# Projecting k from f16 planes with a scale summed ahead, in a graph attention kernel

## The chip, the cores and the metric

The kernel runs on one NeuronCore of a Trainium2 chip. Five engines work from their own instruction queues, each strictly in order: TensorE (PE in the profile, its weight loads PEld), VectorE (DVE), ScalarE (ACT), GpSimd (POOL) and SyncE (SP), which issues most DMA transfers. They wait for each other through semaphores. The metric is the device time of one execution in microseconds (us); the time of a kernel is the median of its runs.

## The reference, cut to what matters

One pre-norm graph attention layer over N = 384 nodes with 1024 features, 16 heads of 64. Each of q, k and v passes two linear layers in a row, all in f32:

```python
h = jnp.maximum(_layernorm(x, axis=-1), 0.0)
q = h @ wq.T + bq
k = h @ wk.T + bk
v = h @ wv.T + bv
q2 = (q @ wiq.T + biq).reshape(N, H, D).transpose(1, 0, 2)
k2 = (k @ wik.T + bik).reshape(N, H, D).transpose(1, 0, 2)
v2 = (v @ wiv.T + biv).reshape(N, H, D).transpose(1, 0, 2)
mask = _build_mask(edge_index, edge_type, edge_type_weights, x.dtype)
scores = jnp.einsum('hnd,hmd->hnm', q2, k2) * scale + mask[None]
attn = jax.nn.softmax(scores, axis=-1)
out = jnp.einsum('hnm,hmd->hnd', attn, v2).transpose(1, 0, 2).reshape(N, OUT_F)
return x + out @ wo.T + bo
```

The mask is a 384 x 384 table, filled from 6,528 edges by scattered writes (a later edge of the same pair wins), with minus infinity where there is no edge.

## The kernel before

**Slots.** The weights come in 56 chunks of 128 x 1024 (512 KB), in the order of `chunks`: eight of Wv (slots w = 0 to 7), eight of Wq (8 to 15), eight of Wiv (16 to 23), eight of Wk (24 to 31), then Wiq and Wik by turns (32 to 47), then eight of Wo. A slot is the work on one chunk.

**Planes.** To keep f32 accuracy, an operand is kept as a high plane and a low plane (what the high one leaves out), and each product is made of three matmuls: high by high, high by low, low by high (`mm3`, lines 456 to 458). There are two kinds. Unscaled planes are fp32r (4 bytes): that is how v, q and k are projected, with `hT` (the normalised, rectified x without its division by sigma, transposed, two fp32r planes) as the moving operand. Scaled planes are f16: the matrix is multiplied by a power of two chosen so that it fits, and for that its size must be known beforehand. `scan_load` brings a chunk ahead of time into a spare buffer, `scan_sum` lets ScalarE sum its absolute values into a column of `l1`, `bound_max(w)` (VectorE) takes the largest of a row of `l1`, and `bound(w)` turns that column on TensorE (a transpose into a PSUM bank of tag "g") and lets VectorE derive the scale t and its reciprocal u (`power`). `BOUNDS` says in which slot each bound is made. Wiv, Wiq and Wo have such scales; so have v and q themselves, whose absolute sums are taken when their banks are emptied (`evac_f`).

**A slot of a projection** (`proj`). First comes `slot_head(w)`: ScalarE splits off the high plane of chunk w+2 (`split_hi`, line 107 unscaled, line 101 scaled), high planes of v or q (`planes_of`), the evacuation of the previous slot's bank (`flush`), a sum (`scan_sum`); then VectorE does `bound_max`, the low plane of chunk w+2 (`split_lo`, line 126 unscaled, line 124 scaled) and the low halves collected in `post`; then SP issues the load of chunk w+5 and the scan's load. Then TensorE does the 24 matmuls of the slot into a bank of tag "g" (three of them); after the matmuls of k = 6 `bound(w)` follows, where there is one, so that TensorE waits there for `bound_max(w)` and the later matmuls of the slot stand behind it.

**k's evacuation** (`evac_row`): VectorE multiplies the bank by `rrow`, the row of 1/sigma (line 479); ScalarE adds the bias and rounds to the high plane (line 480); VectorE makes the low plane (line 481, one slot later through `post`).

**Beside it.** VectorE compares edges with each other for the mask (`mask_detect`, `mask_index`), GpSimd scatters their values (`mask_scatter`, two a slot, 51 in all), loads the three tables back (`mask_load`, in slots 29 to 31), and adds the output bias to the residual in six pieces (`residual_add`, line 599, one in each of the slots 26 to 31, behind that slot's scatters). Neither waits for TensorE. In the k stage v2 is also scaled: its maxima (`v2_max`, line 659), a bound in slot 26 (`v2_scale`), and one evacuation a slot from slot 27 on (`v2_evac`, lines 694 and 695). In the v stage GpSimd clears `kz`, the buffer for the low planes of k2.

**After the projections** `fill_qk` does slots 32 to 47 with `qk_head` at their head; the first 84 units of it (28 k steps) run before the attention loop, the rest between its steps. The results of slots 32 and 33 are copied into stacked layouts by DMA (line 752), and then the attention's first score matmul (line 901) can go.

Of the kernel before, what the change touches and what calls it, by code (L numbers as in the profile page):

```python
# [12 lines left out]
PSC = 32768.0  # L13
BF16 = mybir.dt.bfloat16
# [12 lines left out]
def gnn_kernel(ctx: ExitStack, tc: tile.TileContext, x, edges, erows, etw, wq, wk, wv, wiq, wik, wiv, wo,  # L27
# [18 lines left out]
    WARM = (24,2,0)  # L46
# [34 lines left out]
    def weight_scale(w):  # L81
        return {"iv": u_iv, "iq": u_iq, "o": u_o}.get(chunks[w][0])
# [46 lines left out]
    SCANS = [("iv", i + 3, i + 5) for i in range(8)] + [("iq", i + 13, i + 15) for i in range(8)]  # L129
    SCANS += [("o", i + 25, i + 27) for i in range(8)]  # L130

    def scan_buf(i):
        return scan[:, i % 3, :] if i < 16 else qF3[:, i % 3, :]

    def scan_load(w):
        for i, (n, at, _) in enumerate(SCANS):
            if at == w:
                nc.sync.dma_start(scan_buf(i), W[n][i % 8])

    def scan_sum(w):  # L140
        for i, (n, _, at) in enumerate(SCANS):
            if at == w:
                x = scan_buf(i)
                nc.scalar.activation(x, x, AF.Abs, accum_out=l1[:, 1 + i // 16, i % 8:i % 8 + 1])
# [7 lines left out]
    BOUNDS = {8: 0, 13: 1, 16: 2, 23: 3, 37: 4}  # L152

    def bound_of(w):
        return ((0, t_v, u_v), (1, t_iv, u_iv), (0, t_q, u_q), (1, t_iq, u_iq), (2, t_o, u_o))[BOUNDS[w]]

# [39 lines left out]
    w8, vmax = small[:, 4:16], small[:, 16:24]  # L196
    t_v, u_v, t_iv, u_iv, t_v2, u_v2, t_o, u_o, t_sum, u_sum, t_out = (small[:, c:c + 1] for c in range(24, 35))
    bias_ao, bias_q = small[:, 40:48], small[:, 48:56]
    t_q, u_q, t_iq, u_iq, u_c, neg_c = (small[:, c:c + 1] for c in (35, 36, 37, 38, 39, 56))
    l1 = const.tile([128, 3, 8], F32, name="l1")  # L200
# [276 lines left out]
    def evac_row(ps, hi, lo, bias):  # L477
        f = work.tile([128, N], F32, tag="e", name="f", bufs=EB)
        nc.vector.tensor_tensor(f, ps[:, :N], rrow, OP.mult)
        nc.scalar.activation(hi, f, AF.Identity, bias=bias)  # L480
        post.append(lambda: nc.vector.scalar_tensor_tensor(lo, f, bias, hi.bitcast(F32), op0=OP.add, op1=OP.subtract))
# [22 lines left out]
    def slot_head(w):  # L504
# [3 lines left out]
        if w > 16:  # L508
            planes_of(w - 17, qT, qF, u_q)
# [18 lines left out]
    def proj(src, dst, bidx, extra=None):  # L528
        nonlocal w
        for m in range(8):  # L530
# [22 lines left out]
            else:  # L553
                pend.append(lambda ps=ps, m=m: evac_row(ps, dst[:, 0, m, :], dst[:, 1, m, :],
# [567 lines left out]
```

## Time and profile before

| | |
|---|---|
| time, median of 3 runs | 283.77 us (283.31 to 285.13) |
| profiled execution | 284.17 us |
| its span, first to last instruction | 282.5 us |
| mean granted TensorE clock | 0.999 |
| ScalarE busy | 197.6 us (70%) |
| GpSimd busy | 145.7 us (52%) |
| bytes moved by DMA | 65.69 MB |
| absolute sums of scanned chunks on ScalarE | 16 at 1044 ns and 8 at 1051 ns |

Rows of the profile have this form: line of the kernel, engine, operation, the tile written <- the tiles read, shape, count; then busy time, the mean of one in ns, and the idle time of that engine just before with what ended it. In a timeline the first column is the start and the second the duration, in us. Busy time of TensorE overstates it, since matmuls are pipelined: the distance from one start to the next is what a matmul costs in a stream.

### The profile page before, as it was taken

The numbers are of one execution on the slowest core, as the hardware profiler recorded it, in microseconds if no ns is written. First come the engines' busy times: TensorE is split into PE (matmuls) and PEld (weight loads), VectorE is DVE, ScalarE is ACT, GpSimd is POOL, SyncE is SP. The second block draws the span as 40 slices with busy tenths as digits, with TensorE's granted clock in tenths as the row PEclk, the third lists the DMA queues.
The fourth block names the chain that finished last, engine by engine and source line by source line (L and its number), as shares of the span: only waits on it lengthen the run. The fifth ranks groups of instructions, "written<-read, shape, count | busy, mean of one in ns | idle before, by whom it ended". The sixth has DMA issues, their size and how long they took to land. (4 is left out here: it accounts for less than half of the span.)

```text
span 282.5 us, 5050 instructions
## 1 busy us (share of the span) xinstructions
PE 275.7 (98%) x1630; PEld 218.0 (77%) x1630; DVE 222.4 (79%) x515; ACT 197.6 (70%) x393; POOL 145.7 (52%) x170
## 2 busy tenths in 40 slices
PE   7999999999999999999999999999999999999994
PEld 6899999999954447999977887878778695655443
DVE  3948965885869754999989987898988889999423
ACT  3786887795989644243986878687888897777510
POOL 3857565458778676899003435447373732332210
PEclk9999999999999999999999999999999999999999
DMA  7799999999668841477993689999988989522105
GB/s 265 235 319 404 372 387 404 342 363 338 243 216 303 319 134 62 149 277 224 363 353 76 212 261 225 231 223 194 213 203 190 227 227 255 113 69 48 35 19 206
DMA packets 45562, 65.69 MB, mean 233 GB/s; under 512 B 26592, under 2 KB 32224, under 8 KB 45536
## 3 DMA queue, kind: packets, MB, share of 16 engines
q1 hardware_dynamic: 43152, 63.18, 72.9%
q0 software_dynamic: 2064, 1.80, 2.3%
q10 hardware_dynamic: 320, 0.39, 0.5%
q8 instruction: 13, 0.21, 0.3%
q14 instruction: 13, 0.11, 0.1%
HBM read 50.36 MB, written 3.39 MB: 190 GB/s over the span
## 5 line engine op out<-in xcount | busy, mean ns | idle before, releaser
L456 PE MATMUL g<-g,whl 128*128 128x384 f32 (+1 forms) x312 | 105.4, 338 | 0.0
L458 PE MATMUL g<-g,whl 128*128 128x384 f32 (+1 forms) x312 | 104.0, 333 | 0.2 <-DVE whl L126 0.2
L457 PE MATMUL g<-g,whl 128*128 128x384 f32 (+1 forms) x312 | 103.8, 333 | 0.0
L313 POOL DMA_INDIRECT tab<-edge x51 | 59.5, 1167 | 31.8 <-DMA tab<-edge 14.4
L458 PEld LDWEIGHTS g<-g,whl 128*128 128x128 f32 x248 | 46.5, 188 | 0.5 <-DVE whl L126 0.5
L456 PEld LDWEIGHTS g<-g,whl 128*128 128x128 f32 x248 | 46.6, 188 | 0.4
L457 PEld LDWEIGHTS g<-g,whl 128*128 128x128 f32 x248 | 46.6, 188 | 0.0
L126 DVE TENSOR_TENSOR whl<-raw,whl 128x1024 fp32r<-128x1024 f32 x23 | 33.6, 1459 | 7.5 <-ACT whl L107 7.2
L107 ACT ACTIVATE whl<-raw 128x1024 fp32r<-128x1024 f32 (+1 forms) x38 | 33.6, 890 | 4.7 <-DMA raw<-in_wv_dram 2.2
L910 DVE CUSTOM_DVE_ANT_0 e<-s,ma,small 128x384 f32<-128x384 f32 x48 | 29.0, 606 | 1.6 <-PE s L902 1.2
L915 ACT ACTIVATE e<-e,s 128x384 f32<-128x384 f32 x48 | 29.1, 607 | 0.5 <-DVE s L910 0.4
L101 ACT ACTIVATE whl<-raw,small 128x1024 f16<-128x1024 f32 (+1 forms) x28 | 25.7, 925 | 4.1 <-PE g L458 4.0
L950 ACT ACTIVATE pt<-e,s 128x384 f16<-128x384 f32 x21 | 12.9, 612 | 17.4 <-POOL s L938 17.4
L942 POOL TENSOR_TENSOR e<-e,s 128x384 f32<-128x384 f32 x21 | 17.3, 825 | 11.9 <-DVE s L935 10.3
L124 DVE SCALAR_TENSOR_TENSOR whl<-raw,small,whl 128x1024 f16<-128x1024 f32 x16 | 21.0, 1312 | 3.0 <-ACT whl L101 2.6
L112 POOL TENSOR_TENSOR whl<-raw,whl 128x256 fp32r<-128x256 f32 x20 | 18.1, 912 | 8.7 <-ACT whl L107 8.7
L901 PE MATMUL s<-ks,qs 128*128 128x384 f32 x48 | 20.8, 433 | 0.4 <-DVE s L910 0.3
L991 POOL TENSOR_TENSOR g<-aof,g 128x384 f16<-128x384 f32 x8 | 7.4, 924 | 23.8 <-ACT g L990 23.8
L126 POOL TENSOR_TENSOR whl<-raw,whl 128x1024 fp32r<-128x1024 f32 x3 | 7.8, 2612 | 22.7 <-ACT whl L107 22.7
L456 PEld LDWEIGHTS <-g 128*128 128x128 f16 x100 | 9.8, 98 | 11.7 <-issue 3.1
L954 DVE SCALAR_TENSOR_TENSOR pt<-e,s,pt 128x384 f16<-128x384 f32 x21 | 15.7, 749 | 3.3 <-ACT pt L950 3.3
L458 PEld LDWEIGHTS <-g 128*128 128x128 f16 x100 | 9.8, 98 | 10.9
(184 smaller groups left out, 555.7 us busy)
## 6 DMA issues: line engine op xcount, KB each, us to landing
raw<-in_wv_dram SPq DMA_DIRECT2D x8, 512.0 KB
raw<-in_wq_dram SPq DMA_DIRECT2D x8, 512.0 KB
scan<-in_wiv_dram SPq DMA_DIRECT2D x8, 512.0 KB
raw<-in_wiv_dram SPq DMA_DIRECT2D x8, 512.0 KB
scan<-in_wiq_dram SPq DMA_DIRECT2D x8, 512.0 KB
raw<-in_wk_dram SPq DMA_DIRECT2D x8, 512.0 KB
raw<-in_wiq_dram SPq DMA_DIRECT2D x8, 512.0 KB
raw<-in_wik_dram SPq DMA_DIRECT2D x8, 512.0 KB
```

The source lines that it names most:

```text
L101: soon(j if parts > 1 else -1, lambda c=c: nc.scalar.activation(hi[:, c], raw[w][:, c], AF.Copy, scale=sc))
L107: soon(j if parts > 1 else -1, lambda c=c: nc.scalar.activation(hi[:, c], raw[w][:, c], AF.Copy))
L112: nc.gpsimd.tensor_tensor(lo, raw[w][:, c:c + D // 4], hi.bitcast(F32), OP.subtract)
L124: nc.vector.scalar_tensor_tensor(lo, raw[w], sc, hi, op0=OP.mult, op1=OP.subtract)
L126: (eng or nc.vector).tensor_tensor(lo, raw[w], hi.bitcast(F32), OP.subtract)
L313: nc.gpsimd.indirect_dma_start(out=tabs[c // RNG], out_offset=bass.IndirectOffsetOnAxis(ap=idx[:, c:c + 1], axis=0), in_=val[:, c:c + 1], ...
L456: nc.tensor.matmul(ps, lhi, rhi, start=first, stop=False)
L457: nc.tensor.matmul(ps, lhi, rlo, start=False, stop=False)
L458: nc.tensor.matmul(ps, llo, rhi, start=False, stop=last)
L901: nc.tensor.matmul(ps[:, :N], qs[:, o, c], ks[:, o, :], start=True, stop=False)
L910: nc.vector.tensor_tensor_reduce(e, st_ps.pop(i)[:, :N], ma[:, t, :], neg_c, 3.0e38, OP.add, OP.min, s[:, t:t + 1])
L915: nc.scalar.activation(es[i], es[i], AF.Exp, bias=s[:, t:t + 1], scale=-1.0, accum_out=s[:, 3 + t:4 + t])
```

## The change

Wk joins the matrices with a scale: its eight chunks are scanned in slots 11 to 18 and summed in slots 13 to 20, its bound is made in slot 21, and its chunks are then split into f16 planes. The scans of Wiq move from slots 13 to 20 to slots 18 to 25, its bound from slot 23 to slot 29; the bound of q moves from slot 16 to 17, the planes of q from slots 17 to 24 to slots 18 to 25, and the scan buffers are dealt out accordingly. Wo's scan keeps its slots, but its eighth load, in slot 32, is now issued too (`scan_load` in `qk_head`); before only seven were.

The moving operand becomes eight pairs of f16 planes, `hk`, of h with its division by sigma, times 1024. They are made by VectorE in slots 4 to 20 (`h_planes`): add the two planes of `hT`, multiply by 1024 and `rrow`, copy to f16, subtract for the low plane. So the bank needs no row of 1/sigma: `evac_k` reads it with ScalarE (scale and bias), copies to the high plane with ScalarE, and leaves VectorE the low plane. `hk` lies in the buffers of `nat` and `kz`; `kz` is cleared after the k projection, and the early copy of v2 goes to the tag "qs".

```diff
+HSC = 1024.0
...
-    WARM = (24,2,0)
+    WARM, H0 = (24, 2, 0), 4
...
     def weight_scale(w):
-        return {"iv": u_iv, "iq": u_iq, "o": u_o}.get(chunks[w][0])
+        return {"iv": u_iv, "iq": u_iq, "o": u_o, "k": u_k}.get(chunks[w][0])
...
-    SCANS = [("iv", i + 3, i + 5) for i in range(8)] + [("iq", i + 13, i + 15) for i in range(8)]
-    SCANS += [("o", i + 25, i + 27) for i in range(8)]
+    SCANS = sorted([(n, i + c, i + c + g, i) for n, c, g in (("iv", 3, 2), ("k", 11, 2), ("iq", 18, 2), ("o", 25, 2)) for i in range(8)], key=lambda c: c[1])
+    SROW = {"iv": 1, "k": 2, "iq": 1, "o": 2}
...
-    BOUNDS = {8: 0, 13: 1, 16: 2, 23: 3, 37: 4}
+    BOUNDS = {8: 0, 13: 1, 17: 2, 21: 5, 29: 3, 37: 4}
...
     def colmm(ps, w, src, k):
         hi, lo = whl[w]
-        mm3(ps[:, :N], hi[:, k * 128:(k + 1) * 128], lo[:, k * 128:(k + 1) * 128],
-            src[:, 0, k, :], src[:, 1, k, :], k == 0, k == KT - 1)
+        a, b = src[k] if isinstance(src, list) else (src[:, 0, k, :], src[:, 1, k, :])
+        mm3(ps[:, :N], hi[:, k * 128:(k + 1) * 128], lo[:, k * 128:(k + 1) * 128], a, b, k == 0, k == KT - 1)
...
-    def evac_row(ps, hi, lo, bias):
+    def evac_k(ps, hi, lo, bias):
         f = work.tile([128, N], F32, tag="e", name="f", bufs=EB)
-        nc.vector.tensor_tensor(f, ps[:, :N], rrow, OP.mult)
-        nc.scalar.activation(hi, f, AF.Identity, bias=bias)
-        post.append(lambda: nc.vector.scalar_tensor_tensor(lo, f, bias, hi.bitcast(F32), op0=OP.add, op1=OP.subtract))
+        nc.scalar.activation(f, ps[:, :N], AF.Identity, bias=bias, scale=s_k)
+        nc.scalar.activation(hi, f, AF.Copy)
+        post.append(lambda: nc.vector.tensor_tensor(lo, f, hi.bitcast(F32), OP.subtract))
...
         planes_of(w - 9, vT, vF, u_v)
-        if w > 16:
-            planes_of(w - 17, qT, qF, u_q)
+        if w > 17:
+            planes_of(w - 18, qT, qF, u_q)
...
         while post:
             post.pop(0)()
+        h_planes(w)
         load(w + 5)
         scan_load(w)
...
-        if w == 23:
+        if w == 21:
+            nc.vector.tensor_scalar(s_k, t_k, 1.0 / HSC, None, op0=OP.mult)
+        if w == 29:
             nc.vector.tensor_tensor(u_c, u_q, u_iq, OP.mult)
...
+    def h_planes(w):
+        k, s = divmod(w - H0, 2)
+        if s == 0 and 0 <= k < KT:
+            hs[k] = work.tile([128, N], F32, tag="e", name="hs", bufs=EB)
+            nc.vector.tensor_tensor(hs[k], hT[:, 0, k, :].bitcast(F32), hT[:, 1, k, :].bitcast(F32), OP.add)
+        if s == 1 and 0 <= k < KT:
+            nc.vector.scalar_tensor_tensor(hs[k], hs[k], HSC, rrow, op0=OP.mult, op1=OP.mult)
+        if s == 0 and 0 <= k - 1 < KT:
+            f = hs.pop(k - 1)
+            nc.vector.tensor_copy(hk[k - 1][:, 0, :], f)
+            nc.vector.tensor_tensor(hk[k - 1][:, 1, :], f, hk[k - 1][:, 0, :], OP.subtract)
...
     def extra_v(m):
-        if m in (3, 4):
-            nc.gpsimd.memset(kz.bitcast(F32)[64 * (m - 3):64 * (m - 3) + 64, :, 4 - m, :], 0.0)
         detect(m)
...
-        if m == 1:
+        if m == 2:
             vhl = big.tile([128, NT, 2 * NP, 2, 64], F16, tag="g4", name="vhl")
...
-    proj(hT, kT, 1, extra_k)
+    proj([(t[:, 0, :], t[:, 1, :]) for t in hk], kT, 1, extra_k)
     flush(True)
+    kz = work.tile([128, 2, 2, N], F32R, tag="kz", name="kz", bufs=1)
+    for j in range(2):
+        nc.gpsimd.memset(kz.bitcast(F32)[64 * j:64 * j + 64, :, 1 - j, :], 0.0)
...
         load(w + 5)
+        scan_load(w)
         scan_sum(w)
```

More of the change, by code (lines that the diff above doesn't have):

```diff
@@ L199, in gnn_kernel @@
     t_q, u_q, t_iq, u_iq, u_c, neg_c = (small[:, c:c + 1] for c in (35, 36, 37, 38, 39, 56))
+    t_k, u_k, s_k = (small[:, c:c + 1] for c in (13, 14, 15))
     l1 = const.tile([128, 3, 8], F32, name="l1")
@@ L558, in proj @@
             w += 1
[L560 removed]
+    hk = []
+    for j in range(2):
+        t = work.tile([128, 2, N], F32R, tag="nat", name="hk", bufs=2).bitcast(F16)
+        hk += [t.rearrange("p a n -> p (a n)").rearrange("p (k a n) -> p k a n", k=2, a=2)[:, k, :, :] for k in range(2)]
+    t = work.tile([128, 2, 2, N], F32R, tag="kz", name="hkz", bufs=1).bitcast(F16)
+    hk += [t.rearrange("p a b n -> p (a b n)").rearrange("p (k a n) -> p k a n", k=4, a=2)[:, k, :, :] for k in range(4)]
+    hs = {}
+    def h_planes(w):
[9 more added lines that the diff above has]
+            nc.vector.tensor_tensor(hk[k - 1][:, 1, :], f, hk[k - 1][:, 0, :], OP.subtract)
     def extra_v(m):
[L563 to L564 removed]
         detect(m)
```

23 lines of the change are left out of this document (12 added, 11 removed).

## The prediction, made before the result was known

> **What bounds the kernel now.** I read the page first, then TensorE's records in order of time, then busy time cut by slots (a slot is one weight chunk, numbered w as in the code), then the records of VectorE (DVE) and GpSimd (POOL) in the slots where TensorE stumbles, and last the chain of waits. The page and TensorE's timeline:
>
> ```profile
> span 282.5 us, 5050 instructions
> ...
> PE 275.7 (98%) x1630; PEld 218.0 (77%) x1630; DVE 222.4 (79%) x515; ACT 197.6 (70%) x393; POOL 145.7 (52%) x170
> ```
> ```profile
> 113.93 0.33 PE L456 MATMUL g<-g,whl 128*128 128x384 f32 x1
> ...
> 118.09 0.33 PE L456 MATMUL g<-g,whl 128*128 128x384 f32 x1
> ...
> 135.55 0.44 PE L458 MATMUL g<-g,whl 128*128 128x384 f32 x1 [0.17 <-DVE whl L126]
> ...
> 143.66 0.34 PE L456 MATMUL g<-g,whl 128*128 128x384 f16 x1
> ...
> 147.44 0.47 PE L456 MATMUL g<-g,whl 128*128 128x384 f32 x1
> ...
> 158.82 0.33 PE L901 MATMUL s<-ks,qs 128*128 128x384 f32 x1
> ```
>
> TensorE is never idle for long, so what counts is the step from matmul to matmul. The first two records open slots 25 and 26 of the k projection (slots 24 to 31, 24 matmuls each): 118.09 - 113.93 = 4.16 us, 173 ns a matmul in f32. The fourth and fifth open slot 32, the same 24 matmuls with f16 planes, and slot 33: 147.44 - 143.66 = 3.78 us, 158 ns. The third is a stumble in slot 30, released by VectorE's low plane of that chunk (L126). The last is the first matmul of the attention. Cut by slots 28 to 30 (columns: PE, PEld, DVE, ACT, POOL busy, clock, DMA share):
>
> ```profile
> 126.55:130.71 4.16, 4.16 (x25) 4.16 (x25) 4.16 (x3) 2.18 (x4) 4.14 (x4) 1.00 0.64 200
> 130.71:134.87 4.16, 4.16 (x25) 4.16 (x25) 4.16 (x4) 1.42 (x3) 3.65 (x4) 1.00 0.90 281
> 134.87:139.50 4.63, 4.46 (x26) 4.14 (x26) 4.63 (x8) 4.07 (x8) 0.00 (x0) 1.00 1.00 365
> ```
>
> Slot 30 takes 4.63 instead of 4.16: the stumble costs 0.5. In these slots VectorE is as full as TensorE, in the first two with three or four operations a slot. Its records say why, beside GpSimd's:
>
> ```profile
> 111.24 0.68 DVE L659 TENSOR_REDUCE small<-tv 128x1 f32<-128x512 f32 x1
> ...
> 117.68 2.94 DVE L126 TENSOR_TENSOR whl<-raw,whl 128x1024 fp32r<-128x1024 f32 x1
> 120.55 0.60 DVE L481 SCALAR_TENSOR_TENSOR g<-f,bc,g 128x384 fp32r<-128x384 f32 x1
> 121.54 1.21 DVE L126 TENSOR_TENSOR whl<-raw,whl 128x1024 fp32r<-128x1024 f32 x1
> ...
> 123.21 0.28 DVE L147 TENSOR_REDUCE small<-g 128x1 f32<-128x128 f32 x1
> ...
> 124.86 0.14 DVE L673 SCALAR_TENSOR_TENSOR small<-small 128x1 f32<-128x1 f32 x1
> ...
> 125.39 3.75 DVE L126 TENSOR_TENSOR whl<-raw,whl 128x1024 fp32r<-128x1024 f32 x1
> ...
> 135.95 0.74 DVE L695 SCALAR_TENSOR_TENSOR vhl<-s,small,vhl 128x512 f16<-128x512 f32 x1
> ...
> 140.49 1.29 DVE L124 SCALAR_TENSOR_TENSOR whl<-raw,small,whl 128x1024 f16<-128x1024 f32 x1 [0.55 <-ACT whl L101]
> ```
> ```profile
> L599 POOL TENSOR_TENSOR res<-res,bot 128x512 f32<-128x512 f32 x6 | 8.6, 1437 | 0.1
> ```
> ```profile
> 118.23 1.30 POOL L599 TENSOR_TENSOR res<-res,bot 128x512 f32<-128x512 f32 x1
> ...
> 126.07 1.30 POOL L599 TENSOR_TENSOR res<-res,bot 128x512 f32<-128x512 f32 x1
> ...
> 128.18 2.12 POOL L599 TENSOR_TENSOR res<-res,bot 128x512 f32<-128x512 f32 x1
> ...
> 133.10 1.31 POOL L599 TENSOR_TENSOR res<-res,bot 128x512 f32<-128x512 f32 x1
> ```
>
> The low plane costs 1.21 us alone, 2.94 and 3.75 when GpSimd adds the output bias to the residual meanwhile (six adds, 8.6 us, first and last at 118.23 and 133.10). VectorE loses about what the add lasts: 2.94 - 1.21 = 1.7 for 1.30; 3.75 - 1.21 = 2.5 for 1.30 and part of 2.12. Rule and row differ here. The Trainium skill (SBUF — State Buffer, "SBUF: two separate sides") says that VectorE, with two SBUF operands, and GpSimd lock one port pair, and that whoever starts first keeps it for the whole instruction. L126 started first at 117.68 and still lost, so I go by the row; the rule's own outcome is the first rival.
>
> **The change, part by part.** *Matmuls.* Eight slots from 4.16 to 3.78: 8 x 0.38 = 3.0 us, and the stumble of 0.5 goes if its cause does. That is all that TensorE can gain.
>
> *VectorE in the k projection.* The old evacuation had VectorE multiply each bank by the row of 1/sigma and make the low half; now ScalarE reads the bank and only a low half is left, about 0.60 (nearest row L481). The scaled low plane of Wk is 1.29 instead of 1.21. So VectorE gets lighter. But the bound of Wiq moves from slot 23 to slot 29, and TensorE, which works in order, does its transpose after the seventh k of slot 29. The transpose needs `bound_max(29)`, which VectorE reaches only behind everything queued ahead. From the start of slot 24 that is: six v2_max at 0.68 (4.1), low planes of chunks 26 to 30 at 1.29 (6.5), two q low planes and four low halves at 0.60 (3.6), the v2 bound and scale from 123.21 to 125.00 (1.8), two v2 low halves at 0.74 (1.5), v2_top, five small steps like those of the scale (0.7). Sum 18.2; records overlap by 0.07 (117.68 + 2.94 against 120.55), some 24 times, so 16.5. VectorE can begin when ScalarE's first copy has landed:
>
> ```profile
> 109.83 0.60 ACT L655 ACTIVATE tv<-g 128x512 f32<-128x512 f32 x1 [6.21 <-issue]
> ```
>
> 110.4 + 16.5 = 126.9, if GpSimd were silent. Adds that wait for nothing on TensorE fall where they fell: three lie wholly before 127.4 (+3.9, to 130.8), then the one of 2.12 (132.9), then the fifth (134.2), and part of the sixth. So `bound_max(29)` comes at 134.2 to 135.2. TensorE is there after five slots of 3.78, six eighths of a sixth and two transposes (0.2): slot 24 opens one f32 slot and a transpose before slot 25, at 113.93 - 4.16 - 0.1 = 109.7, and 109.7 + 18.9 + 2.8 + 0.2 = 131.6. It waits 2.6 to 3.6; I take 3.0. Behind it in TensorE's queue stand the rest of slot 29 and all that follows. In the kernel before, the same place is passed at 130.71 + 0.75 x 4.16 = 133.8; now at 134.6. The lead of 2.2 us is gone, and two slots of 3.78 instead of 4.63 and 4.16 (1.2 less) only make that good again: slot 32 opens at 134.6 + 0.9 + 7.6 + about 0.5 for a bank (next part) = 143.6, against 143.66.
>
> *ScalarE behind the moved bound.* `split_hi(32)` needs u_iq and stands in slot 30's head ahead of the evacuation of slot 29, whose bank slot 31 wants (three banks, one taken by the transpose). u_iq comes after one more low plane, two low halves and the scale: 134.7 + 1.29 + 0.60 + 0.74 + 0.9 = 138.2. From there ScalarE is full:
>
> ```profile
> 139.32 1.14 ACT L101 ACTIVATE whl<-raw,small 128x1024 f16<-128x1024 f32 x1
> ...
> 142.48 1.05 ACT L107 ACTIVATE whl<-raw 128x1024 fp32r<-128x1024 f32 x1
> ...
> 143.99 0.67 ACT L694 ACTIVATE vhl<-t,small 128x512 f16<-128x512 f32 x1
> ...
> 147.56 1.33 ACT L101 ACTIVATE whl<-raw,small 128x512 f16<-128x512 f32 x2
> ```
> ```profile
> L144 ACT ACTIVATE scan<-scan 128x1024 f32<-128x1024 f32 x16 | 16.7, 1044 | 0.0
> ...
> L466 ACT ACTIVATE nat<-g,bc 128x384 fp32r<-128x384 f32 x8 | 4.5, 564 | 1.0 <-PE g L458 1.0
> ...
> L990 ACT ACTIVATE g<-aof 128x384 f16<-128x384 f32 x8 | 4.2, 519 | 0.1
> ```
> ```profile
> 154.79 0.47 ACT nat L466
> ...
> 155.86 2.49 DMA ks<-nat
> ```
>
> Up to the split of chunk 34 (147.56 before) it has 1.14 + 1.05, three evacuations at 0.56 + 0.52 (now two passes), three v2 high halves at 0.67, two sums at 1.04 and 0.19: 9.9, less eleven overlaps of 0.09: 8.9. 138.2 + 8.9 = 147.1. The chain of waits begins there: the evacuation at 154.79 and the copy of 2.49 at 155.86 let the attention's first matmul go at 158.82, which TensorE reaches as the data land. So the entry moves by -0.5 to +0.5, and the matmuls after it are those of before.
>
> *h planes.* Eight times an add, a multiply by 1/sigma, a copy to f16 and a low plane on VectorE, in slots 4 to 20. Nearest rows: 0.60 for each two-operand step, at most 0.41 for the copy:
>
> ```profile
> L432 DVE CAST whl<-raw 128x512 fp32r<-128x512 f32 x1 | 0.4, 412 | 0.0
> ```
> ```profile
> 15.40:78.40 63.00, 63.00 (x366) 62.74 (x364) 46.18 (x147) 51.89 (x95) 37.87 (x43) 1.00 0.96 351
> 78.40:109.70 31.30, 31.30 (x149) 14.37 (x147) 20.01 (x47) 20.19 (x33) 23.06 (x23) 1.00 0.65 225
> ```
>
> 8 x 2.2 = 17.7 us, 1.0 a slot: 12.5 in the v and q stages, where VectorE has 63.0 - 46.2 = 16.8 free, 5 in the iv stage, where 11.3 are free. The low planes are queued two slots ahead, and that hides it: nothing on the path, and if the cover failed, up to the 1.0 a slot. Its side effect is that the last index of the mask comes up to 3 us later, and the scatters and adds on GpSimd with it.
>
> *Sums and loads.* Eight sums of Wk, 1.2 each, on ScalarE in slots 13 to 20 (free there: 11.1 in v and q, 11.1 in iv); those of Wiq run until slot 27. The added loads are 4 MB; five instead of three fall into the q stage, where the queues are at 0.96: 1.05 MB at 351 GB/s, 3.0 us of transfer behind loads issued three slots ahead. The eighth load of Wo is new (seven were issued), 0.5 MB in slot 32 on SP's queue ahead of the stack copies; a load takes some 1.5 us by 351 GB/s. Wk's bound at the end of slot 21 leaves two slots for two splits of 2.4. The clearing of kz goes to GpSimd after the last k matmul, ten us ahead of its use. I take nothing for any of these; uncovered, the loads would cost 1.5 to 3.
>
> **Sum.** -3.0 for the matmuls, +3.0 for the wait at the bound, -0.5 for the stumble, +0.5 for the bank: 0.0, and +-1.0 by the spread of the wait (2.6 to 3.6) and of the entry (+-0.5). The span stays at 282.5. The profiled execution took 284.17 (span and 1.7 around it), 0.4 over the median of 283.77; I state the forecast on the median: 283.8, alone 282.8 to 284.8.
>
> **Rivals.** *The gain arrives* (18%). If VectorE loses little to the adds, `bound_max(29)` is there by 131.6 and u_iq by 135. For it: 126.9 without any loss. Against it: 2.94 and 3.75. Price -3.0 and -0.5, of which the entry's chain may keep 0.2: 280.5. By the first-starter rule of the Trainium skill, cited above, the low planes would stay at 1.2 and the time would come out here; the trace does not bear it out.
>
> *The moved bound holds ScalarE* (20%), slower. Place: `split_hi(32)`. Once u_iq is later than 138.7, each us is a us at the entry, for ScalarE has no gap from there on. If each of the six adds costs 2.1 (the fourth's length) instead of 1.3, or later scatters push them behind slot 29, u_iq comes at 142: +3.4, 287.2. For it: the 3.75, and the later index. Against it: five of the six adds lasted 1.3.
>
> *The clock falls in the new wait* (8%). After the last matmuls the granted clock drops:
>
> ```profile
> 277.00:280.00 3.00, 1.61 (x15) 1.20 (x13) 0.97 (x2) 0.00 (x0) 0.00 (x0) 1.00 0.65 237
> 280.00:282.00 2.00, 0.00 (x0) 0.00 (x0) 0.00 (x0) 0.00 (x0) 0.00 (x0) 0.93 0.19 65
> ```
>
> TensorE is busy for 1.61 of the first stretch, so it ends near 278.6, and the mean over the last stretch is 0.93: at half clock that is 0.3 us, so the drop came some 3 us after the last matmul, about the length of my wait. Half speed for as long as the wait adds half of 3.0: 285.3. The Trainium skill (TensorE: Matmul & The Clock Gate, "What's actually happening") puts the idle window at about 3.4 us; by that most of my waits escape it.
>
> **Chances.** Forecast 54%, gain 18%, held ScalarE 20%, clock 8%. One per cent (2.8 us, about what a measurement of this kernel tells from no change) puts the gain into faster, forecast and clock into the same. The range 280.3 to 286.6 takes in the forecast, the clock, the gain and the start of the held case.
>
> **What would show it.** Slots 24 to 28 at 3.78. A gap of about 3 us in TensorE in slot 29, released by VectorE, with residual adds beside long low planes. ScalarE waiting in slot 30 for u_iq and full afterwards. First attention matmul at 158 to 160. Wrong: no gap in slot 29, the attention opening before 156.5, or gaps in slots 4 to 23, which would mean that the h planes have no cover.

## The result, and the profile after

The changed kernel takes 282.23 us (median of 7 runs, 281.56 to 285.85) against 283.80 (283.31 to 285.13) of the kernel before on the same chip: a ratio of 0.9932, 95% interval 0.9909 to 0.9956. In a later series on another chip it was 281.75 against 284.26, 0.9920 (0.9895 to 0.9944). So the change makes the kernel 0.7 to 0.8% faster, some 2 us, where 283.8, no change, was forecast. Medians here are over all runs; the ratios leave out runs in a slower state with a lower granted clock, such as the longest of these seven (285.85 us at 0.992). The profiled execution has a span of 280.3 us, 2.2 less than before.

From the page, the span, and among the costliest groups the scatters of GpSimd (POOL) with their idle time:

```profile
span 280.3 us, 5120 instructions
...
L316 POOL DMA_INDIRECT tab<-edge x51 | 61.7, 1210 | 40.8 <-DMA tab<-edge 27.2
```

The same group in the page of the kernel before:

```profile
L313 POOL DMA_INDIRECT tab<-edge x51 | 59.5, 1167 | 31.8 <-DMA tab<-edge 14.4
```

GpSimd now waits 27.2 us for scatters to land, before 14.4. TensorE's timeline, with the openings of slots 25, 26, 32 and 33, the transpose in slot 29 that was to wait, and the first matmul of the attention:

```profile
113.86 0.33 PE L459 MATMUL g<-hk,whl 128*128 128x384 f16 x1
...
117.76 0.33 PE L459 MATMUL g<-hk,whl 128*128 128x384 f16 x1
...
132.98 0.27 PE L167 MATMUL g<-ident,small 128*128 128x128 f32 x1
...
141.37 0.33 PE L459 MATMUL g<-g,whl 128*128 128x384 f16 x1
...
145.14 0.47 PE L459 MATMUL g<-g,whl 128*128 128x384 f32 x1
...
156.52 0.33 PE L927 MATMUL s<-ks,qs 128*128 128x384 f32 x1
```

A slot of the k projection takes 117.76 - 113.86 = 3.90 us, not 3.78. The transpose goes at once, without a wait. Slot 32 opens at 141.37 (143.66 before) and the attention at 156.52 (158.82 before): the 2.3 us won in the k stage reach the attention whole. Slots 28 to 30 by windows (columns as before):

```profile
125.67:129.56 3.89, 3.89 (x25) 2.35 (x24) 2.54 (x2) 3.86 (x8) 3.31 (x3) 1.00 0.91 331
129.56:133.57 4.01, 4.01 (x27) 2.48 (x25) 3.84 (x6) 3.88 (x8) 3.52 (x4) 1.00 0.84 297
133.57:137.47 3.90, 3.90 (x26) 2.35 (x24) 3.73 (x8) 2.36 (x4) 3.85 (x4) 1.00 0.94 315
```

No gap of TensorE in any of them; VectorE (third busy column) has 1.35 us free in slot 28. Its timeline says why, and the next two fences show GpSimd's adds and ScalarE:

```profile
127.02 2.39 DVE L125 SCALAR_TENSOR_TENSOR whl<-raw,small,whl 128x1024 f16<-128x1024 f32 x1 [2.37 <-ACT whl L102]
129.33 0.55 DVE L484 TENSOR_TENSOR g<-f,g 128x384 fp32r<-128x384 f32 x1
129.80 0.74 DVE L717 SCALAR_TENSOR_TENSOR vhl<-s,small,vhl 128x512 f16<-128x512 f32 x1
130.46 0.14 DVE L162 TENSOR_REDUCE small<-l 128x1 f32<-128x8 f32 x1
130.78 1.28 DVE L125 SCALAR_TENSOR_TENSOR whl<-raw,small,whl 128x1024 f16<-128x1024 f32 x1 [0.17 <-ACT whl L102]
131.98 1.62 DVE L484 TENSOR_TENSOR g<-f,g 128x384 fp32r<-128x384 f32 x1
...
134.88 0.16 DVE L152 RECIPROCAL small<-small 128x1 f32<-128x1 f32 x1
135.07 1.37 DVE L530 TENSOR_TENSOR small<-small 128x1 f32<-128x1 f32 x1
```
```profile
127.04 1.27 POOL L621 TENSOR_TENSOR res<-res,bot 128x512 f32<-128x512 f32 x1
...
131.55 1.63 POOL L621 TENSOR_TENSOR res<-res,bot 128x512 f32<-128x512 f32 x1
...
134.49 1.29 POOL L621 TENSOR_TENSOR res<-res,bot 128x512 f32<-128x512 f32 x1
```
```profile
122.03 0.67 ACT L482 ACTIVATE f<-g,bc,small 128x384 f32<-128x384 f32 x1 [0.71 <-PE g L461]
...
123.77 1.04 ACT L146 ACTIVATE g<-g 128x1024 f32<-128x1024 f32 x1
...
124.81 1.04 ACT L146 ACTIVATE g<-g 128x1024 f32<-128x1024 f32 x1
...
125.85 1.13 ACT L102 ACTIVATE whl<-raw,small 128x1024 f16<-128x1024 f32 x1
...
135.07 1.15 ACT L102 ACTIVATE whl<-raw,small 128x1024 f16<-128x1024 f32 x1 [1.60 <-DVE small L152]
...
144.22 1.32 ACT L102 ACTIVATE whl<-raw,small 128x512 f16<-128x512 f32 x2
```

L162 is `bound_max(29)`: 130.46, 2.5 us ahead of the transpose, where 134.2 to 135.2 was forecast. VectorE had even run out of work: it idled 2.37 us until ScalarE's high plane of chunk 30 (125.85 + 1.13). ScalarE came to that plane behind the evacuation of slot 26's bank, for which it waited for TensorE until 122.03, and behind two sums (L146). And the first residual add falls at 127.04, not at 118.23; only that one lies ahead of the bound. L152 (134.88) is u_iq; ScalarE waits 1.60 for it, and the split of chunk 34 comes at 144.22 (147.56 before).

### The profile page after: what moved, and what is told of

It reads as the page before. It is cut to its first block, busy times and chain, and to the rows that moved or that the text cites. A ratio compares the mean times of both kernels' runs of the same rounds, so it can differ in the third digit from the quotient of the medians.

```text
span 280.3 us, 5120 instructions
## 1 busy us (share of the span) xinstructions
PE 273.9 (98%) x1631; PEld 204.0 (73%) x1631; DVE 230.6 (82%) x545; ACT 210.6 (75%) x417; POOL 146.4 (52%) x170
## 5 line engine op out<-in xcount | busy, mean ns | idle before, releaser
L459 PE MATMUL g<-g,whl 128*128 128x384 f32 (+1 forms) x248 | 83.8, 338 | 0.0
L316 POOL DMA_INDIRECT tab<-edge x51 | 61.7, 1210 | 40.8 <-DMA tab<-edge 27.2
L461 PE MATMUL g<-g,whl 128*128 128x384 f32 (+1 forms) x248 | 82.5, 333 | 0.0
L460 PE MATMUL g<-g,whl 128*128 128x384 f32 (+1 forms) x248 | 82.4, 332 | 0.0
L102 ACT ACTIVATE whl<-raw,small 128x1024 f16<-128x1024 f32 (+1 forms) x36 | 34.8, 971 | 7.9 <-DVE small L528 5.3
L125 DVE SCALAR_TENSOR_TENSOR whl<-raw,small,whl 128x1024 f16<-128x1024 f32 x24 | 32.4, 1350 | 6.4 <-ACT whl L102 6.4
L459 PEld LDWEIGHTS g<-g,whl 128*128 128x128 f32 x184 | 34.6, 188 | 0.3
L460 PEld LDWEIGHTS g<-g,whl 128*128 128x128 f32 x184 | 34.6, 188 | 0.0
L461 PEld LDWEIGHTS g<-g,whl 128*128 128x128 f32 x184 | 34.5, 188 | 0.0
L108 ACT ACTIVATE whl<-raw 128x1024 fp32r<-128x1024 f32 (+1 forms) x30 | 25.2, 848 | 1.4 <-DMA raw<-in_wv_dram 1.4
L146 ACT ACTIVATE scan<-scan 128x1024 f32<-128x1024 f32 x23 | 24.0, 1044 | 0.0
L127 DVE TENSOR_TENSOR whl<-raw,whl 128x1024 fp32r<-128x1024 f32 x15 | 19.4, 1293 | 2.4 <-ACT whl L108 2.3
L459 PEld LDWEIGHTS <-whl 128*128 128x128 f16 x128 | 12.5, 97 | 11.0 <-issue 4.4
L461 PEld LDWEIGHTS <-whl 128*128 128x128 f16 x128 | 12.5, 98 | 8.2
```

The lines of the kernel that those rows point to most:

```text
L102: soon(j if parts > 1 else -1, lambda c=c: nc.scalar.activation(hi[:, c], raw[w][:, c], AF.Copy, scale=sc))
L108: soon(j if parts > 1 else -1, lambda c=c: nc.scalar.activation(hi[:, c], raw[w][:, c], AF.Copy))
L125: nc.vector.scalar_tensor_tensor(lo, raw[w], sc, hi, op0=OP.mult, op1=OP.subtract)
L127: (eng or nc.vector).tensor_tensor(lo, raw[w], hi.bitcast(F32), OP.subtract)
L146: nc.scalar.activation(x, x, AF.Abs, accum_out=l1[:, SROW[n], k:k + 1])
L316: nc.gpsimd.indirect_dma_start(out=tabs[c // RNG], out_offset=bass.IndirectOffsetOnAxis(ap=idx[:, c:c + 1], axis=0), in_=val[:, c:c + 1], ...
```

## The experiments

The theory that the two profiles suggest: the shorter step of TensorE is the whole gain; it arrives because `bound_max(29)` is early; that in turn is so because the adds came late, held back through the scatters by the added loads (A). Rival: the adds matter little wherever they fall (B). A third suspicion: late mask tables or late stack copies decide at the attention's first matmul (C).

All kernels side by side. The times in the middle are starts in the profiled execution, in us: slot 24 opens, first residual add, `bound_max(29)`, u_iq (L152 or its line), first stack copies of k issued by SyncE (SP), first matmul of the attention; then from the opening of slot 24 to the end of the last matmul. Openings of slot 24 lie up to 1 us apart in runs that do not touch the slots before it, so the last column compares best.

| kernel | median (runs) | ratio to before, 95% | slot 24 | add | bound | u_iq | copies | attention | 24 to end |
|---|---|---|---|---|---|---|---|---|---|
| before | 283.80 (7) | | 109.66 | 118.23 | | | 155.32 | 158.82 | 168.95 |
| changed | 282.23 (7) | 0.9932, 0.9909-0.9956 | 109.96 | 127.04 | 130.46 | 134.88 | 153.22 | 156.52 | 166.69 |
| a_again | 281.75 (6) | 0.9920, 0.9895-0.9944 | 109.59 | 127.67 | 130.07 | 133.62 | 151.91 | 156.19 | 166.22 |
| b_f16 | 282.90 (10) | 0.9966, 0.9941-0.9991 | 110.38 | 116.89 | | | 153.54 | 156.81 | 166.95 |
| b_no_adds | 284.13 (10) | 0.9991, 0.9973-1.0009 | 110.12 | none | | | 153.23 | 158.81 | 168.24 |
| a_no_adds | 282.00 (6) | 0.9909, 0.9878-0.9940 | 110.56 | none | 129.97 | 134.59 | 151.64 | 157.12 | 166.13 |
| a_no_wiq_scan | 282.82 (10) | 0.9954, 0.9933-0.9975 | 110.05 | 121.29 | 129.46 | 135.22 | 153.20 | 156.61 | 166.38 |
| a_no_wk_scan | 283.01 (8) | 0.9952, 0.9932-0.9972 | 110.20 | 124.21 | 130.68 | 136.16 | 153.41 | 156.77 | 166.16 |
| a_no_scans | 283.72 (10) | 0.9971, 0.9939-1.0002 | 110.36 | 120.42 | 132.76 | 137.95 | 155.02 | 157.94 | 167.99 |
| a_low_x2 | 282.32 (5) | 0.9944, 0.9906-0.9982 | 109.55 | 126.64 | 131.39 | 135.31 | 152.41 | 156.11 | 166.50 |
| a_low_x4 | 287.47 (4) | 1.0106, 1.0059-1.0153 | 110.18 | 128.26 | 135.51 | 141.62 | 158.69 | 161.91 | 171.81 |
| a_adds_early | 283.89 (12) | 0.9983, 0.9963-1.0002 | 109.99 | 123.98 | 130.46 | 134.86 | 156.72 | 159.63 | 170.91 |
| a_adds_iv | 284.93 (12) | 1.0022, 0.9989-1.0055 | 112.08 | 92.80 | 131.99 | 136.45 | 153.54 | 158.73 | 166.29 |
| a_adds_dve | 281.75 (6) | 0.9911, 0.9889-0.9933 | 110.32 | none | 129.74 | 134.35 | 151.41 | 156.88 | 166.14 |

Medians of the changed kernel's family stand beside those of before in their own series (283.80, 284.21, 284.38, 284.26); the ratio takes that in.

### Where the gain comes from: b_f16, a_no_adds, b_no_adds

**b_f16**, the kernel before with nothing changed but the form of the k matmuls:

```diff
...
+        a, b = src[:, 0, k, :], src[:, 1, k, :]
+        if chunks[w][0] == "k":
+            hi, lo = hi.bitcast(F16), lo.bitcast(F16)
+            a, b = a.bitcast(F16)[:, :N], b.bitcast(F16)[:, :N]
...
```

> The kernel before, in which only the matmuls of the k projection read f16 halves of the same planes (k's values are meaningless). It prices the matmul step alone, with the adds and VectorE's evacuation as before. Theory: slots without a stall take 3.90 us (162.5 ns a matmul), but VectorE's low planes of slots 30 to 32 are late as before, so that TensorE stalls 1.5 to 2.5 us there and gains 0 to 0.8 us in all: 283.0 to 283.8. Rival (the step alone is the gain): 281.2 to 281.9.

Its slots are 3.90 us, none stumbles, and from slot 24 to the end it takes 166.95, 2.0 less than the kernel before, against 2.26 less for the whole change. Up to the attention's first matmul it takes 46.43 from there, the kernel before 49.16 and the changed kernel 46.56. So the step alone brings nearly all that the profiled executions gain (the ratios, 0.9966 and 0.9932, have overlapping intervals). Neither expectation holds whole: the stalls of the theory do not come, and the median, 282.90, lies between the two ranges. Its adds fall as early as 116.89, and TensorE still never waits for a low plane: two low planes take 1.22 and 2.31, those of chunks 29 and 30 1.93 and 1.81, where the kernel before had 3.75 and 2.16. The loss per add depends on what it falls on; the last section has the rows.

**a_no_adds**, the changed kernel without the adds, and **b_no_adds**, the kernel before without them:

```diff
-        if m >= 2:
-            residual_add(m - 2)
```

> The changed kernel without the six adds of the output bias to the residual, so the output lacks that bias. Theory (u_iq sets the entry, and the adds still cost it about 1.1 us through the low plane at 127.02): u_iq's last step at 133.8 instead of 134.9, first attention matmul at 155.4, 281.1 us. Rival (the adds cost the changed kernel nothing): first attention matmul at 156.5, 282.2 us. In both no gap in slot 29.

> The kernel before without the six adds of the output bias to the residual, so the output lacks that bias. Theory (the adds cause the stumble of slot 30 and the spread of the runs): slot 30 at 4.16 like its neighbours, first attention matmul at 158.3, 283.5 us with a spread under 0.6, that is 1.5 us above the changed kernel without adds (282.0). Rival (the stumble has another cause): slot 30 stays at 4.5 or more, 283.8 us or more with the old spread.

Of b_no_adds, slot 30 takes 4.16 like its neighbours: without the adds the stumble is gone. The rest of that theory does not come true: the median, 284.13, is that of the kernel before beside it (284.26), and the runs still spread over 1.13 us. Of a_no_adds, the attention opens 157.12 - 110.56 = 46.56 after slot 24, exactly as in the changed kernel (156.52 - 109.96), although u_iq comes 0.9 earlier by that measure: the rival holds, u_iq does not set the entry there. Between the two kernels, 168.24 - 166.13 = 2.11 us are won, about eight slots at 4.16 - 3.90. That is the change without anything beside it. VectorE of a_no_adds ahead of the bound:

```profile
127.62 1.28 DVE L125 SCALAR_TENSOR_TENSOR whl<-raw,small,whl 128x1024 f16<-128x1024 f32 x1 [2.37 <-ACT whl L102]
128.82 0.55 DVE L484 TENSOR_TENSOR g<-f,g 128x384 fp32r<-128x384 f32 x1
129.31 0.75 DVE L717 SCALAR_TENSOR_TENSOR vhl<-s,small,vhl 128x512 f16<-128x512 f32 x1
129.97 0.15 DVE L162 TENSOR_REDUCE small<-l 128x1 f32<-128x8 f32 x1
```

With no add at all VectorE waits the same 2.37 us for ScalarE, and the bound stands at 129.97, or 129.4 on the changed kernel's clock (slot 24 opens 0.60 later here). That is the silent value that the forecast put at 126.9.

### Why the adds came late: a_no_wiq_scan, a_no_wk_scan, a_no_scans

The scan loads of Wiq, of Wk, or of both are not issued:

```diff
-            if at == w:
+            if at == w and n != "iq":
```
```diff
-            if at == w:
+            if at == w and n != "k":
```
```diff
-            if at == w:
+            if at == w and n not in ("iq", "k"):
```

> The changed kernel without the eight scan loads of Wiq (their sums run over what the buffers hold, so u_iq is another power of two). Theory (those loads, now in slots 18 to 25, hold up the landing of the scatters): the waits of GpSimd for tab<-edge after 100 us shrink to under 2 us in all, the first add starts near 118 to 121 instead of 127, a gap of 0.5 to 2.5 us opens in slot 29, 282.7 to 284.5. Rival (VectorE's h planes hold GpSimd up): the first add stays near 127, no gap, 282.2.

> The changed kernel without the eight scan loads of Wk (slots 11 to 18; their sums run over what the buffers hold). If Wk's loads delay the scatters: the delay of 1.2 to 2.7 us that the scatters have between 63 and 100 us goes, and the first add starts near 124 to 125. If only Wiq's late loads count for the big delay, the first add still starts after 124. Time 282.2 +- 0.6 in either case.

> The changed kernel without the sixteen loads that feed the sums of Wk and Wiq; their sums read what lies in the buffers, so u_k and u_iq, and all that is scaled by them, are meaningless. Leaving out Wiq's loads alone brought the first residual add from 127.0 to 121.3, Wk's alone to 124.2; together about 118.4, where it fell in the kernel before (118.2). The forecast's theory (the adds, where they fell before, push bound_max(29) to 134): bound_max(29) at 133 to 135, TensorE waits 1 to 2.5 us in slot 29, first attention matmul at 158 or later, 283.5 us or more. The rival (the bound is reached by about 130.5 wherever the adds fall, because VectorE idles 2.4 us ahead of it anyhow): bound_max(29) at 131.5 or earlier, no gap over 0.3 in slot 29, first attention matmul at 156 to 157, 282.0 to 282.9 us.

The first add moves from 127.04 to 121.29, 124.21 and, with both left out, 120.42; the wait for scatters to land falls from 27.2 to 18.2 us there. So the loads hold 6.6 of the 8.8 us, and what is left to 118.23 is no more than 2.2. The windows of the changed kernel and of the one before from 102 to 110 us show the queues (last two columns: DMA share and GB/s):

```profile
102.00:110.00 8.00, 8.00 (x40) 3.67 (x38) 4.44 (x9) 5.28 (x8) 4.39 (x5) 1.00 0.67 233
```
```profile
102.00:110.00 8.00, 8.00 (x40) 3.84 (x38) 1.81 (x3) 1.73 (x3) 5.39 (x6) 1.00 0.36 118
```

Yet in none of the three does TensorE wait in slot 29. Without Wiq's loads, where the theory expected a gap of 0.5 to 2.5 us, two adds lie wholly ahead of the bound and a third begins ahead of it, and the bound comes 19.41 us after slot 24 opens, just as without any add:

```profile
127.11 1.28 DVE L125 SCALAR_TENSOR_TENSOR whl<-raw,small,whl 128x1024 f16<-128x1024 f32 x1 [2.11 <-ACT whl L102]
...
129.46 0.15 DVE L162 TENSOR_REDUCE small<-l 128x1 f32<-128x8 f32 x1
```
```profile
125.99 1.28 POOL L621 TENSOR_TENSOR res<-res,bot 128x512 f32<-128x512 f32 x1
```

Without Wk's loads the first add comes where it was expected and the bound at 130.68, 20.48 after slot 24 against 20.50 in the changed kernel; the median, 283.01, lies just above the range of 281.6 to 282.8.

VectorE and GpSimd of a_no_scans, where the adds lie nearly where they fell in the kernel before:

```profile
127.42 3.21 DVE L125 SCALAR_TENSOR_TENSOR whl<-raw,small,whl 128x1024 f16<-128x1024 f32 x1 [2.37 <-ACT whl L102]
130.55 1.62 DVE L484 TENSOR_TENSOR g<-f,g 128x384 fp32r<-128x384 f32 x1
132.10 0.74 DVE L717 SCALAR_TENSOR_TENSOR vhl<-s,small,vhl 128x512 f16<-128x512 f32 x1
132.76 0.14 DVE L162 TENSOR_REDUCE small<-l 128x1 f32<-128x8 f32 x1
```
```profile
125.16 1.29 POOL L621 TENSOR_TENSOR res<-res,bot 128x512 f32<-128x512 f32 x1
...
127.62 1.28 POOL L621 TENSOR_TENSOR res<-res,bot 128x512 f32<-128x512 f32 x1
...
129.71 2.05 POOL L621 TENSOR_TENSOR res<-res,bot 128x512 f32<-128x512 f32 x1
...
132.53 1.28 POOL L621 TENSOR_TENSOR res<-res,bot 128x512 f32<-128x512 f32 x1
```

Neither expectation of a_no_scans holds whole. The bound moves to 132.76 (132.4 on the changed kernel's clock), 3.0 later than without adds: the low plane loses 3.21 - 1.28 = 1.93 and L484 1.62 - 0.55 = 1.07. The adds that lie ahead of 127 cost nothing, since VectorE waits for ScalarE there anyhow. TensorE reaches its transpose at about 133.4 in this run (132.98 + 0.40) and does not wait. But the next low plane and low half lose to the adds too (2.31 and 1.61 us), and they stand ahead of the scale: u_iq comes at 137.95, the copies are issued at 155.02, and the attention's first matmul waits for them:

```profile
157.94 0.41 PE L927 MATMUL s<-ks,qs 128*128 128x384 f32 x1 [0.85 <-DMA ks<-nat]
```

It opens 47.58 after slot 24 instead of 46.56, and the median is 283.72 beside 284.38 of the kernel before: the ratio, 0.9971, no longer differs clearly from 1, though the loss stands at the entry and not in slot 29. So A holds in part: the loads do push the adds back, and that keeps u_iq early, but TensorE does not wait in slot 29 with earlier adds either, and for that wait B is right.

### What a later bound costs: a_low_x2, a_low_x4

The low plane of chunk 30 is made twice, or four times:

```diff
-        split_lo(w + 2)
+        for _ in range(4 if w == 28 else 1):
+            split_lo(w + 2)
```

> The changed kernel with the low plane of chunk 30 computed twice in slot 28; the result is the same. bound_max(29) moves from 130.5 to 131.8, still ahead of TensorE (132.7): both theories expect no gap over 0.3 in slot 29. Theory (from u_iq on, the entry follows it us for us, with 0.3 us to spare): first attention matmul at 157.3 to 157.6, behind the stack copies, 283.0 to 283.3 us. Rival (the entry has more to spare than one low plane): 156.5, 282.2 us.

> The changed kernel with the low plane of chunk 30 computed four times in slot 28 instead of once: three more VectorE operations of about 1.2 us ahead of bound_max(29), the result the same. bound_max(29) should come at about 134.1 (130.5 + 3.6). TensorE asks for it at about 132.6, so both theories expect a gap of about 1.5 in slot 29. The forecast's chain (u_iq late by 3.6, ScalarE full from there to the split of chunk 34): first attention matmul at 159.5 to 160.2, and 285.3 to 286.0 us, more than the gap. The rival (the entry is set by TensorE's own matmuls, the late u_iq hides): first attention matmul later by the gap alone, 157.9 to 158.2, and 283.6 to 284.0 us.

With two, the bound at 131.39 and u_iq 0.8 later than in the changed kernel (25.76 after slot 24, not 24.92) leave the attention at 46.56 after slot 24: there was more to spare than 0.3, as the rival had it (the median, 282.32, is near the 282.2 that it named). With four, the operations meet the adds and the bound moves by 5.05 us, not 3.6; TensorE's wait comes where the forecast saw it:

```profile
135.80 0.36 PE L167 MATMUL g<-ident,small 128*128 128x128 f32 x1 [2.43 <-DVE small L162]
135.95 0.53 PE L459 MATMUL g<-hkz,whl 128*128 128x384 f16 x1
136.27 0.53 PE L460 MATMUL g<-hkz,whl 128*128 128x384 f16 x1
...
161.91 0.41 PE L928 MATMUL s<-ks,qs 128*128 128x384 f32 x1 [0.72 <-DMA ks<-nat]
```

After 2.43 us of idling, matmuls go 0.32 us apart instead of 0.16. Windows over that wait and the stretch behind it (granted clock third from the end):

```profile
133.20:135.80 2.60, 0.17 (x3) 0.04 (x2) 2.60 (x5) 0.50 (x2) 2.42 (x2) 1.00 0.51 158
135.80:138.80 3.00, 3.00 (x10) 1.48 (x11) 3.00 (x2) 0.00 (x0) 2.97 (x3) 0.52 0.65 224
138.80:141.80 3.00, 3.00 (x18) 1.77 (x17) 2.88 (x7) 0.00 (x0) 2.98 (x3) 0.92 0.89 295
```

So the price of a late bound is the wait, a clock halved for 3.4 us (granted clock 0.50 from 135.90 to 139.30), and then another wait for the copies at the entry: 171.81 - 166.69 = 5.1 us, for a bound that comes about 5 later. The median, 287.47, lies above both expectations, which had neither the longer delay nor the clock. From u_iq to the issue of the copies it takes 158.69 - 141.62 = 17.07 us here and 155.02 - 137.95 = 17.07 in a_no_scans; from the issue to the first matmul 3.2 and 2.9. In these two runs the entry follows u_iq us for us.

### Where else the adds could lie: a_adds_early, a_adds_iv, a_adds_dve, and the changed kernel again

**a_adds_early** moves the adds ahead, between the scatters of slots 25 to 28:

```diff
+        if m == 1:
+            residual_add(0)
+        if m == 2:
+            residual_add(1)
...
+        scatters(1)
...
-        if m >= 2:
-            residual_add(m - 2)
```

> The changed kernel with the six residual adds put one or two slots earlier in GpSimd's order, between the scatters. Theory (the place of the adds decides): they land near 118 to 133 us as in the kernel before, VectorE reaches bound_max(29) near 134, TensorE waits 1 to 2.5 us after the seventh k of slot 29, and the time is 283.2 to 284.7. Rival (the lighter evacuation alone keeps VectorE in time): the adds land early too, but no gap over 0.5 us in slot 29, and 282.2 +- 0.5.

The bound stays at 130.46 and slot 29 has no gap, although the first add falls at 123.98. But every add delays the scatters behind it (the last goes at 141.17, in the changed kernel at 133.35), the mask tables land late, and VectorE sits in front of its mask selection:

```profile
150.33 2.77 DVE L329 COPY_PREDICATED ma<-mbs 128x1152 f32<-128x1152 int32 x1 [3.48 <-DMA mbs<-tab]
```

The low halves for the stacks stand behind it; the copies go at 156.72, the first matmul of the attention at 159.63 after a wait of 2.50. That is the third suspicion, C. So the rival is right about slot 29, and the median, 283.89, lies in the theory's range for a reason that neither had. The profiled execution took 286.26, the longest of the twelve, so its waits are longer than those of a usual one.

**a_adds_iv** puts them in slots 17 to 22:

```diff
-        scatters(2)
+        scatters(1)
+        if 1 <= k < 7:
+            residual_add(k - 1)
+        scatters(1)
...
-        if m >= 2:
-            residual_add(m - 2)
```

> The changed kernel with the six residual adds one a slot in slots 17 to 22, between that slot's two scatters, instead of slots 26 to 31. Theory (the adds lie in the time in which GpSimd waits for a scatter to land, and VectorE has room there): TensorE's slots 16 to 23 as in the changed kernel, last mask load earlier by 3 us or more, u_iq at 133.8, first attention matmul 155.4 to 156.5, 281.1 to 282.2 us. Rival (VectorE has too little room in these slots: 24.8 us of 31.3 are busy and each add costs it 1.3 to 2.5): gaps of 0.5 to 3 us in slots 17 to 23 released by low planes, and 282.7 to 285 us.

The rival was right in its price (284.93) and in the length of the gap, but what releases the gap is the bound of Wk in slot 21 and not a low plane. VectorE loses its time there too (a step of the h planes takes 2.10, a copy 1.90):

```profile
104.16 0.32 PE L167 MATMUL g<-ident,small 128*128 128x128 f32 x1 [1.92 <-DVE small L162]
```

Slot 21 takes 6.12 instead of 4.00, and slot 24 opens at 112.08. That is the forecast's mechanism, in another slot.

**a_adds_dve** gives the adds to VectorE, two each in slots 21 to 23, behind that bound; **a_again** is the changed kernel, in the same series:

```diff
-        nc.gpsimd.tensor_tensor(y, y, bob[i % 2], OP.add)
+        nc.vector.tensor_tensor(y, y, bob[i % 2], OP.add)
...
         bounds(w)
+        if k >= 5:
+            residual_add(2 * k - 10)
+            residual_add(2 * k - 9)
...
-        if m >= 2:
-            residual_add(m - 2)
```

> The changed kernel with the six residual adds on VectorE instead of GpSimd, two each in slots 21, 22 and 23 behind the transpose of that slot; nothing is left out. Theory (VectorE idles 1.7, 1.6 and 1.7 us in these slots, an add alone takes about 0.68 us, and the k projection is then free of adds): no new gap in slots 21 to 24, u_iq at about 134.0, the stack copies issued 1.5 us or more earlier than in the changed kernel, first attention matmul at 156.5, 281.9 us with a spread under 0.5 us, as without the adds. Rival (the adds push the low planes of chunks 23 to 25 or the two-operand operation is slowed by GpSimd's scatters): gaps of 0.3 to 1 us in slots 22 to 25, 282.4 to 283.2 us.

> The changed kernel as it is, beside the next three on one chip. Theory (its adds fall at places that shift from run to run with the landing of the scatters, and the stack copies have only some 0.3 us to spare ahead of the first attention matmul): median 282.2 to 283.2 us, with some runs from 284 to 286.5 us. Rival (the spread of the earlier series was the chip's): all runs within 0.7 us.

An add on VectorE takes 0.68, TensorE has no gap in slots 21 to 25, and the copies leave at 151.41, 5.5 us ahead of the matmul that needs them (3.3 in the changed kernel). The median is 281.75, the same as a_again's on that chip, so it is not faster; its six runs lie within 0.46 us (281.54 to 282.00), a_again's within 1.55 (281.18 to 282.73). The wide spread expected of a_again, up to 284 and above, did not come in its six runs, so how much of the earlier spread was the chip's stays open.

## Why the prediction was wrong

**The step that failed** is the sum for `bound_max(29)`: "Adds that wait for nothing on TensorE fall where they fell: three lie wholly before 127.4 (+3.9, to 130.8)", and with two and a part behind it 134.2 to 135.2. Measured, 130.46. It failed in three places.

- *What an add costs.* Each was charged its length, 7.3 to 8.3 in all. An add costs that only where VectorE has no idle time behind it before the bound. In the changed kernel one add costs 2.39 - 1.28 = 1.1; in a_no_wiq_scan adds at 121.29 and 125.99 cost the bound nothing; with the adds near their old place (a_no_scans) they cost it 3.0.
- *The silent sum.* 126.9 was the sum of VectorE's own operations. Without any add the bound stands at 129.4, because the low plane of chunk 30 cannot start before ScalarE's high plane, done at 127.0. ScalarE came to that plane only at 125.85: the bank of slot 26, which it empties first, is ready at 122.03, and two sums of 1.04 stand behind it, the first of them a moved one of Wiq, which had been taken at nothing.
- *Where the adds fall.* They wait for nothing on TensorE, but they stand behind scatters on GpSimd, and there GpSimd waits for earlier scatters to land. With the loads of Wk and Wiq in the queues that wait rose from 14.4 to 27.2 us and the first add moved by 8.8 us; without those loads it is back within 2.2. The prediction had the added loads at nothing and the adds "up to 3 us later".

So the true sum is 129.4 + 1.1 = 130.5, and with the adds of a_no_scans 129.4 + 3.0 = 132.4. TensorE asks at 132.98, so the first two points alone are enough to take the wait away; the third only makes the margin wider and u_iq earlier.

**TensorE's arrival** was put at 131.6 and is 132.98: the slots are 0.12 longer than thought (0.7 over 5.9 slots), 21 of 24 matmuls stand ahead of the transpose, not 18 (0.5), and slot 24 opened 0.26 later than worked out. Alone this would have left a wait of 1.2 to 2.2.

**The matmuls** were mis-sized: "Eight slots from 4.16 to 3.78: 8 x 0.38 = 3.0 us". It is 8 x 0.26 = 2.1 (a_no_adds against b_no_adds: 2.11). The 3.78 was read where an f16 slot is followed by an f32 one; there the next record begins some 0.12 early and lasts 0.47 instead of 0.33. Slots 32 and 33 together take 8.10 us both before and after.

**The stumble** went, and the adds have their part in it, as said: 4.16 in slot 30 without them. They are not enough for it: b_f16 has them and does not stumble.

**The entry.** "Each us is a us at the entry" is right once u_iq is late: with u_iq at 137.95 (a_no_scans) the attention opens 20.0 us later, and the forecast had 158.8 for 138.2, 20.6 later. But u_iq came at 134.88, ahead of the point from which it decides, and TensorE opens the attention in its own order. That the kernel before opened it "as the data land" was wrong: its record at 158.82 shows no idle time before it, and in b_no_adds the copies leave 5.6 us ahead of that matmul, and it opens no earlier than by the stumble.

**The h planes** are hidden, as said: slots 4 to 23 have no gap, and slot 24 opens at 109.96 against 109.66, within the scatter of the runs.

**The rivals.** The gain that arrives was the outcome, with some 2 us and not the 3.3 of its price, since the matmuls were mis-sized for it too. The forecast gave it on the condition that VectorE loses little to the adds; VectorE does lose little, because most of what an add takes falls into its idle time, and in the changed kernel also because the adds come late. The rule of the Trainium skill (SBUF — State Buffer, "SBUF: two separate sides"), that whoever starts first keeps the pair, is borne out by some rows here and not by others. L125 at 130.78 began 0.77 ahead of the add at 131.55 and kept its 1.28, the add took 1.63, and L484, begun inside it at 131.98, took 1.62 instead of 0.55; but L126 at 117.68 in the kernel before began 0.55 ahead of its add and took 2.94. The held ScalarE and the fallen clock are real, and both appear in a_low_x4, where the bound is late enough (ScalarE waits 8.12 us for u_iq there); in the changed kernel it is not.

What stays open: the spread of the changed kernel's first series (281.56 to 285.85), of which only one execution of 282.02 was profiled. In that profile slot 37 takes 5.79, against 5.21 without adds; there the attention waits 0.34 us for later stack copies (at 167.22). Such a wait stands in b_f16 too (0.72, at 167.89) and in no run without adds on GpSimd, but which add would hold the copies up is not shown.

## What to carry to other kernels

An operation that waits for nothing on the critical engine can still move: follow what stands ahead of it on its own queue, down to the transfers, before keeping its old place in a sum. A queue's sum of durations is a lower bound for its end; look for the operand that paces it from another engine, because the idle time in front of that operand swallows what is added earlier. And take the step of a stream inside a run of one form, never across a change of form.

## What the runs showed of the hardware

- Whether a low plane on VectorE (128x1024, alone 1.27 to 1.29 us in f16 and 1.21 in fp32r) loses to an add on GpSimd goes in these runs by their starts. In the nine cases in which it began 0.73 to 1.02 us ahead of the add, it kept its time and the add took 1.40 to 1.94 instead of 1.27 to 1.31. In the ten in which it began less than that ahead of the add (0.68 us to 0), it lost: 0.24 us in one case, 1.1 or more in the others. Why the border lies at 0.7 and not at zero is not shown.
- Very small VectorE operations can be stretched too: L530, one element per partition, took 1.37 us in the changed kernel at 135.07, begun inside the add of 134.49 to 135.78, and 0.16 without adds. L150 to L152, inside the same add, kept 0.15 to 0.16. L717 and its like, which read PSUM, keep 0.74 to 0.75 beside an add: in a_no_scans the one at 132.10 overlaps the add that begins at 132.53.
- A wait of 2.43 us (a_low_x4) or 2.50 (a_adds_early) brought half clock for 3.4 us; one of 1.92 (a_adds_iv) did not. The windows of a_adds_early show it late, with the wait in the first line:

```profile
156.70:159.60 2.90, 0.43 (x3) 0.11 (x2) 2.84 (x4) 2.64 (x5) 0.00 (x0) 1.00 0.94 271
159.60:162.60 3.00, 2.97 (x13) 2.32 (x14) 2.97 (x6) 2.39 (x5) 1.72 (x1) 0.74 0.57 197
162.60:165.60 3.00, 3.00 (x15) 1.61 (x13) 2.42 (x7) 1.92 (x5) 1.27 (x1) 0.69 0.56 119
```

TensorE resumed there at full rate and slowed at 161.06, 1.4 us later, until 164.47. The Trainium skill (TensorE: Matmul & The Clock Gate, "What's actually happening") has a window of about 3.4 us that runs freely, so that its phase is a matter of chance. The traces agree: the clock rises first at 6.19 in a_low_x4 and at 7.46 in a_adds_early, and it falls 129.71 and 153.60 us later, 38 and 45 times 3.413; it stays down for 3.41 both times. They do not bear out that only a wait as long as such a window brings half clock: in the 3.41 us that ended with the fall, TensorE had idled 2.43 us (a_low_x4) and 1.98 (a_adds_early). In a_adds_iv, with the steps counted from its rise at 5.07, 1.8 us of the wait lay in the step that ended at 104.06, and the clock did not fall.
